# One mask for a pair of index tiles, and the buffers given up for a third pair

## The chip, the cores and the metric

The kernel runs on one core of a Trainium2 chip. The core has engines with queues of their own: TensorE (PE in the profile, its weight loads PEld), VectorE (DVE), ScalarE (ACT), GpSimd (POOL) and SyncE (SP), whose queue issues every DMA of this kernel. Each engine runs its instructions in the order in which they were written; they wait for each other through semaphores. The metric is the device time of one execution, in microseconds.

## The reference

32 audio clips of 313 frames go through one layer. A tokenizer (a DCT of each frame of 512 samples), an attention layer with eight heads, and a feed-forward layer of another kind than usual: each of 256 hidden units has its own wavelength and phase for each of the 512 features, and its output is a weighted sum over the features of sines and cosines from a table with 4096 entries.

```python
def lookup_sin_cos(theta):
    idx = jnp.mod(jnp.round(theta * (4096 / TWO_PI)), 4096).astype(jnp.int32)
    return sin_t[idx], cos_t[idx]

def ffn(x, W, B_param, attn_cos, attn_sin, proj_cos_w, proj_sin_w):
    theta = x[..., None, :] / (1.0 + jnp.abs(W)) + B_param     # (clip, frame, 256, 512)
    sin_theta, cos_theta = lookup_sin_cos(theta)
    cos_sum = jnp.sum(cos_theta * attn_cos, axis=-1)
    sin_sum = jnp.sum(sin_theta * attn_sin, axis=-1)
    return silu(einsum('bsn,dn->bsd', cos_sum, proj_cos_w)
                + einsum('bsn,dn->bsd', sin_sum, proj_sin_w))

h = dct(frames(x))
h = h + attention(layernorm(h))        # rotated Q and K, softmax times a decay matrix, V,
                                       # a norm per head, a SiLU gate, an output matrix
h = h + ffn(layernorm(h))
```

With 32 x 313 x 256 x 512 angles, and a sine and a cosine of each, the feed-forward layer is most of the work.

## The kernel before, in words

**Sines.** Features lie on the 128 partitions, in four groups of 128 (`NC4`). For one hidden unit and one group, VectorE turns the layernormed features of several clips into int16 table indices with one multiply-add (L610); unit and feature set two scalars of each partition. A tile of indices holds 16 blocks (`SLOT`) of one clip's 313 frames: with 8 clips at hand, two (unit, group) parts; with 4 clips four parts, with 2 clips eight, and with 6 clips two parts, which is 12 blocks. Three more VectorE instructions follow over the whole tile: `mask` (L622) wraps the index into the table and flips its top bit, `quarter` (L630) adds a quarter of the table into a second tile, and `wrap` (L636) wraps that. ScalarE takes the sine of each tile (L643) into a float32 tile `trig`; the second of the two sines is the cosine. TensorE multiplies each block by a 128 x 32 matrix that is zero outside one unit's column of weights (`hot`, loaded at L592), and so sums over features in PSUM banks `pa` (L664). One tile of indices and its partner is called a step below: 2144 of them.

**Rounds.** A ring holds the features of up to four pairs of clips. A round takes 32 units (`UNITS`) for all that are in it; a pair of clips stays for eight rounds. The ring fills slowly: one pair for four rounds, two for six, three for four, four from round 14 on, and it empties in the last six rounds. At a round's end the sums leave through `part` (L681) to device memory (L692), and when a pair of clips has all its sums, `output` projects them and adds the residual.

**Attention.** The attention of each clip (a sequence) is woven into the rounds as features are needed. Two sequences, A and B, run before the first round, with ScalarE taking the copies; so do those that fall in rounds with one pair in the ring. The others use VectorE for them. A sequence does: DCT by `rows` (L273: 12 products, one load of the ring of weights per three), layernorm, transposes (L260), V by `rows`, then twice four heads: Q and K and their swapped copies by `columns` (L288), the rotation (L341, L345, L346), scores (L355), maximum (L363), difference (L372), exponentials (L379, L384), sums (L397), and for each head transposes (L412), product with the decay table (L424) and with V (L430); then gate, norm per head, output matrix, residual (L502) and the second layernorm. GpSimd runs three Newton steps of four instructions for each inverse root (L224 to L227) between a seed on VectorE (L218) and the normalising instruction (L248, L484).

**Order.** The order of every engine's instructions is worked out before the build by the class `Plan`. Each piece of work is added with a key, an engine, an estimated duration, and what it reads and writes. `emit` runs through time on those estimates: on the engine that is free first it issues the ready piece with the lowest key. A DMA's data is taken to arrive 3500 ns after its issue (`LAND`). Keys come from the rounds' progress, and attention's keys are spread so that it is done when its clips enter the ring. The estimates set only the order; on the chip the waits decide the times.

**Buffers.** `ix` 4 index tiles, `trig` 3, `hot` 2 (two units, four groups each), a ring of 3 weight tiles, 2 decay tables, `h` for rows and values, `xn` for layernormed rows, `prob` for four heads, `probT`.

Of the kernel before, what the change touches and what calls it, by code (L numbers as in the profile page):

```python
# [21 lines left out]
P = 128  # L22
# [104 lines left out]
def tile_audio_tower(ctx: ExitStack, tc: tile.TileContext, t: dict, out: bass.AP):  # L127
# [7 lines left out]
    N_RING = 3  # L135
    N_IX, N_TRIG, N_HOT, N_PA = 4, 3, 2, 4
# [15 lines left out]
    class Buffers:  # L152


        def __init__(self, name, pool, psum):
            self.name = name
            self.n_ring = 0

# [4 lines left out]
            self.dec = [sb(f"dec{i}", STEP * (NT - 1) + S) for i in range(2)]  # L163

            self.u = sb("u", NC4, S)
            self.qk = [self.u[:, 2 * i : 2 * i + 2, :] for i in range(2)]
            self.h = sb("h", NT, HOP)
            self.v = self.h
            self.xn = sb("xn", NT, HOP)
            self.xnT = sb("xnT", NC4, S)  # L170
            self.prob = sb("prob", NB, NT, S)
            self.probT = sb("probT", NT, S)
            self.raw = self.probT[:, 0:2, :]
            wide = self.prob.rearrange("p a b s -> p (a b s)")
            self.sq = wide[:, : NT * HOP].rearrange("p (i d) -> p i d", d=HOP)
# [36 lines left out]
    def rsqrt(plan, key, val, r, u, kv, kr, ku):  # L212
# [17 lines left out]
        plan.add(key, "POOL", 3500, newton, (kv,), (kr, ku))  # L230

    def layernorm(plan, key, x):

        for i in range(NT):
            def stats(i=i):
                nc.vector.bn_stats(x.st[:N, i, :], x.h[:N, i, :])  # L236
                nc.vector.bn_aggr(x.mv[:N, i, :], x.st[:N, i, :])
            plan.add(key, "DVE", 850, stats, (x.k("h"),), (x.k("mv", i),))
# [6 lines left out]
        for i in range(NT):  # L245
# [3 lines left out]
                    x.xn[:N, i, :], x.h[:N, i, :], x.mv[:N, i, 0:1], x.lr[:N, i : i + 1],  # L249
                    ALU.subtract, ALU.mult,  # L250
                ),
                (x.k("h"), x.k("mv", i), x.k("lr")), (x.k("xn", i),),
            )

    def transposed(plan, key, x):

        for c in range(NC4):
            def go(c=c):
                for i in range(NT):
                    nc.tensor.transpose(  # L260
                        x.W[:, c, ROW0[i] : ROW0[i] + N], x.xn[:N, i, c * P : (c + 1) * P],
                        ident[:N, :N],
                    )
            plan.add(key, "PE", 800, go, x.every("xn", NT), x.banks(c))
# [28 lines left out]
    def attention(plan, keys, sq, x, eng):  # L293
# [9 lines left out]
        def residual(key, load):  # L303
            for i in range(NT):
                f0 = 1 if i and not load else 0
                d, s = h_d[sq, ROW0[i] + f0 : ROW0[i] + N, :], x.h[f0:N, i, :]
                kd, ks = ("h_d", sq), x.k("h")
                if load:
                    plan.add(key, "SP", DMA_NS, lambda d=d, s=s: nc.sync.dma_start(s, d), (kd,), (ks,))
                else:  # L310
                    plan.add(key, "SP", DMA_NS, lambda d=d, s=s: nc.sync.dma_start(d, s), (ks,), (kd,))

        xns, probs, us = x.every("xn", NT), x.every("prob", NB), x.every("u", 2)
# [3 lines left out]
        copy(plan, step(), eng, NT * HOP, x.h[:N], W3, x.banks(0, 1, 2), (x.k("h"),))  # L317
# [8 lines left out]
        copy(plan, step(), eng, NT * HOP, x.v[:N], W3, x.banks(0, 1, 2), (x.k("h"),))  # L326
        plan.add(step(0), "POOL", 500, lambda: nc.gpsimd.memset(x.v[0:1, : NT - 1, :], 0.0), (),
                 (x.k("h"),))

        for hb in range(H // NB):  # L330
            for g in range(hb * NB // 2, (hb + 1) * NB // 2):
# [8 lines left out]
                plan.add(key, "DVE", 810,  # L340
                         lambda qk=qk: nc.vector.tensor_tensor(qk, x.W[:, 0:2, :S], cos_qk, ALU.mult),  # L341
                         x.banks(0, 1), (kq,))

                def turned(qk=qk):
                    nc.vector.tensor_tensor(x.raw, x.W[:, 2:4, :S], sin_qk, ALU.mult)  # L345
                    nc.vector.tensor_tensor(qk, qk, x.raw, ALU.add)  # L346
                plan.add(key, "DVE", 1640, turned, x.banks(2, 3), (x.k("probT"), kq))
            for hd in range(hb * NB, (hb + 1) * NB):
# [16 lines left out]
                if a == NB - 1:  # L365
# [9 lines left out]
                         (x.k("mx", hd % 2), *x.banks(0, 1, 2)), (x.k("prob", a),))  # L375

            def exps(hb=hb, m=m):
                if eng == "DVE":
                    nc.scalar.activation(x.prob[:N, : NB - 1], x.prob[:N, : NB - 1], AF.Exp)  # L379
                for a in range(NB):  # L380
                    for i in range(NT):
                        last = a == NB - 1
                        if last or eng == "ACT":
                            nc.scalar.activation(  # L384
                                x.prob[:N, a, i, :],
                                x.W[:N, i, :S] if last else x.prob[:N, a, i, :], AF.Exp,
# [567 lines left out]
```

## Time and profile before

| | |
|---|---|
| time, median of 3 runs | 18,893.47 us (18,890.79 to 18,904.49) |
| the profiled execution | 18,894.1 us |
| its span, first to last instruction | 18,892.3 us |
| granted TensorE clock, mean | 0.926 |
| ACT busy | 18,090.3 us (96%), of it sines (L643) 17,547.6 |
| DVE busy | 17,770.2 us (94%), of it index work (L610, L622, L630, L636) 15,729.2 |
| PE busy | 14,803.3 us (78%) |
| POOL busy | 656.5 us (3%) |
| DMA | 783.69 MB, 41 GB/s |

A line of a group gives the kernel line, engine, operation, the tile written and those read with their sizes, how often, then busy time and mean ns of one, then the idle time of that engine just before and what ended it. A line of a wait gives engine, tile and line that waited, what it waited for, total us, times, and the longest. A line of the timeline gives start, duration and the work, and in brackets how long the engine stood before it. Matmuls in float32 appear as two records each.

### The profile page before, as it was taken

How to read it: one execution, taken by the hardware profiler on the slowest of the kernel's cores; microseconds unless marked ns; L12 is line 12 of the kernel's file. 1: busy time of each engine (PE TensorE's matmuls, PEld its weight loads, DVE VectorE, ACT ScalarE, POOL GpSimd, SP SyncE). 2: the span in 40 equal slices, each digit the busy share in tenths (PEclk: the TensorE clock that was granted, in tenths of full speed). 3: DMA queues.
4: the chain of work that ended last, by engine and by line, in shares of the span. 5: the costliest groups of instructions: out<-in, count | busy, mean ns of one | idle time of the engine just before them, and what ended most of it. 6: DMA issues, size and time to landing. Idle time of an engine off the chain costs nothing.

```text
span 18892.3 us, 332980 instructions
## 1 busy us (share of the span) xinstructions
PE 14803.3 (78%) x148864; PEld 6590.0 (35%) x148864; DVE 17770.2 (94%) x15244; ACT 18090.3 (96%) x5026; POOL 656.5 (3%) x1222
## 2 busy tenths in 40 slices
PE   8888888887888887888788888887888788766566
PEld 4433333333333333333333333333333333222222
DVE  5999999999999999999999999999999999889998
ACT  3899999999999999999999999999999999999998
POOL 0000000000000000000000000000000000000000
PEclk8999999999999999999999999999999999889998
DMA  3211111111111111111111111111111111000011
GB/s 96 66 52 48 50 57 47 46 51 47 31 35 37 46 42 41 32 40 46 38 45 39 32 44 41 45 40 36 39 38 46 39 45 35 24 10 25 12 30 46
DMA packets 447834, 783.69 MB, mean 41 GB/s; under 512 B 61601, under 2 KB 116129, under 8 KB 446401
## 3 DMA queue, kind: packets, MB, share of 16 engines
q1 hardware_dynamic: 446400, 762.39, 13.3%
q8 instruction: 1167, 19.12, 0.4%
q14 instruction: 267, 2.18, 0.0%
HBM read 657.51 MB, written 104.66 MB: 40 GB/s over the span
## 4 chain that ended last, share of the span: by engine, by line
DVE 55%; ACT 18%; PE 15%; issue 8%; POOL 3%; DMA 1%; DVEq 0%; SPq 0%; ACTq 0%; POOLq 0%
DVE ix L610 20%; ACT trig L643 18%; DVE ix L630 9%; DVE ix L622 9%; PE pa L664 8%; DVE ix L636 8%; PE a_W L288 3%; PE a_W L273 2%; DVE a_mx L363 1%; DVE a_prob L372 1%; DVE a_sm L397 1%; DVE a_probT L424 1%; DVE a_st L236 1%; PE a_W L355 1%; POOL a_lu L224 1%
## 5 line engine op out<-in xcount | busy, mean ns | idle before, releaser
L643 ACT ACTIVATE trig<-ix 128x5008 f32<-128x5008 int16 (+1 forms) x4288 | 17547.6, 4178 | 442.0 <-PE pa L664 185.5
L664 PE MATMUL pa<-trig,hot 128*32 128x313 f32 x131072 | 10373.1, 462 | 3021.0 <-ACT trig L643 3003.0
L664 PEld LDWEIGHTS pa<-trig,hot 128*32 128x32 f32 x131072 | 4058.5, 116 | 8907.0 <-ACT trig L643 4513.9
L610 DVE TENSOR_SCALAR ix<-xT,f 128x2504 int16<-128x2504 f32 (+3 forms) x5888 | 6673.8, 1184 | 211.9 <-ACT trig L643 205.8
L630 DVE TENSOR_SCALAR ix<-ix 128x5008 int16<-128x5008 int16 (+1 forms) x2144 | 3014.4, 1406 | 201.2 <-DVE ix L622 5.0
L622 DVE TENSOR_SCALAR ix<-ix 128x5008 int16<-128x5008 int16 (+1 forms) x2144 | 3023.7, 1410 | 69.2
L636 DVE TENSOR_SCALAR ix<-ix 128x5008 int16<-128x5008 int16 (+1 forms) x2144 | 3017.3, 1407 | 67.2
L288 PE MATMUL a_W<-a_xnT,a_ring 128*128 128x313 f32 x4960 | 1539.2, 446 | 220.1 <-DVE a_u L341 125.1
L273 PE MATMUL a_W<-a_ring,a_u 128*105 128x512 f32 x2256 | 1101.5, 623 | 120.8 <-DVE a_u L499 53.7
L288 PEld LDWEIGHTS a_W<-a_xnT,a_ring 128*128 128x128 f32 x4960 | 882.9, 191 | 868.2 <-issue 284.7
L430 PE MATMUL a_W<-a_h,a_probT 105*105 105x64 f32 x4464 | 540.6, 270 | 118.0 <-DVE a_probT L424 117.7
L273 PEld LDWEIGHTS a_W<-a_ring,a_u 128*105 128x105 f32 x2256 | 360.2, 174 | 722.8 <-issue 579.0
L430 PEld LDWEIGHTS a_W<-a_h,a_probT 105*105 105x105 f32 x4464 | 476.3, 181 | 386.4 <-issue 194.7
L355 PE MATMUL a_W<-a_u 64*105 64x313 f32 x1488 | 502.8, 466 | 112.0 <-DVE a_prob L372 100.6
L412 PE MATMUL a_W<-ident,a_prob 105*105 105x105 f32 x2232 | 325.9, 284 | 186.7 <-ACT a_prob L384 150.9
L273 PE MATMUL a_W<-a_ring,a_xnT 128*105 128x512 f32 x744 | 380.0, 631 | 50.9 <-DVE a_xnT L210 49.3
L224 POOL TENSOR_TENSOR a_gu<-a_gr 105x24 f32<-105x24 f32 x93 | 69.5, 747 | 10066.3 <-DVE a_gr L218 10061.4
L412 PEld LDWEIGHTS a_W<-ident,a_prob 105*105 105x105 f32 x2232 | 259.4, 185 | 344.9 <-ACT a_prob L384 193.2
L260 PE MATMUL a_W<-ident,a_xn 105*128 105x105 f32 x1116 | 190.2, 298 | 234.8 <-DVE a_xn L248 108.2
L355 PEld LDWEIGHTS a_W<-a_u 64*105 64x105 f32 x1488 | 239.3, 178 | 386.0 <-DVE a_prob L372 152.6
L363 DVE TENSOR_REDUCE a_mx<-a_W 105x3 f32<-105x939 f32 x248 | 280.2, 1130 | 17.7 <-PE a_W L355 17.1
L424 DVE TENSOR_TENSOR a_probT<-a_W,a_dec 105x939 f32<-105x939 f32 x248 | 279.9, 1129 | 13.0 <-PE a_W L412 13.0
(136 smaller groups left out, 3461.9 us busy)
## 6 DMA issues: line engine op xcount, KB each, us to landing
hot<-in_hot SPq DMA_DIRECT2D x672, 256.0 KB
a_dec<-in_decay SPq DMA_DIRECT2D x248, 260.5 KB
a_ring<-in_proj SPq DMA_DIRECT2D x128, 256.0 KB
a_ring<-in_dct SPq DMA_DIRECT2D x124, 256.0 KB
a_ring<-wv_d SPq DMA_DIRECT2D x124, 256.0 KB
a_ring<-in_wq SPq DMA_DIRECT2D x124, 256.0 KB
a_ring<-in_wk SPq DMA_DIRECT2D x124, 256.0 KB
a_ring<-in_wq_s SPq DMA_DIRECT2D x124, 256.0 KB
```

The costliest lines, as they stand in the source:

```text
L273: lambda c=c, i=i, k=k, to=to: nc.tensor.matmul(x.W[:N, to, :], lhsT[:, c, ROW0[i] : ROW0[i] + N], x.ring[k], start=(c == 0), stop=(c == N ...
L288: lambda c=c: nc.tensor.matmul(x.W[:, bank, :S], w[:, c, :], x.xnT[:, c, :], start=(c == 0), stop=(c == NC4 - 1)),
L355: lambda i=i, qk=qk, r0=r0: nc.tensor.matmul(x.W[:N, i, :S], qk[r0 : r0 + DH, 0, ROW0[i] : ROW0[i] + N], qk[r0 : r0 + DH, 1, :], start=Tru ...
L363: lambda m=m: nc.vector.tensor_reduce(m[:N], x.W[:N, :NT, :S], AX.X, ALU.max),
L412: nc.tensor.transpose(x.W[:N, jj, ROW0[i] : ROW0[i] + N], x.prob[:N, a, i, ROW0[j] : ROW0[j] + N], ident[:N, :N],)
L430: nc.tensor.matmul(x.y[:N, i, (hd % 2) * DH : (hd % 2 + 1) * DH], x.probT[:N, jj, ROW0[i] : ROW0[i] + N], x.v[:N, jj, hd * DH : (hd + 1) * ...
L610: nc.vector.tensor_scalar(now["ix", x][:, d0 : d0 + 2 * m * S], now["xT", c][:, 2 * at * S : 2 * (at + m) * S], f[:, 0, c, n + u : n + u + ...
L622: nc.vector.tensor_scalar(tl, tl, LUT - 1, LUT // 2, ALU.bitwise_and, ALU.bitwise_xor)
L630: nc.vector.tensor_scalar(tl[:, :E], now["ix", xs][:, :E], float(LUT // 4), None, ALU.add)
L636: nc.vector.tensor_scalar(tl, tl, LUT - 1, None, ALU.bitwise_and)
L643: nc.scalar.activation(tl[:, :E], now["ix", x][:, :E], AF.Sin, bias=-PI32, scale=ANG)
L664: nc.tensor.matmul(now["pa", p][g * 32 : g * 32 + 32, :S], now["hot", z][:, u, c, k, :], now["trig", w][:, s0 : s0 + S], start=(n == 0 and ...
```

## The change

The three instructions over index tiles become two. `quarter` writes its sum to the second half of a double tile from the unmasked first half, and one `mask` then wraps and flips both halves. The tiles are made once, three double ones in place of four single ones. Room comes from elsewhere: layernorm normalises rows in place, so `xn` is gone, and one buffer `h` holds rows, values and each head's result, tracked in four column groups; `prob` keeps three heads and the fourth's exponentials go to `probT`, so heads are taken in the order 3, 2, 0, 1; one decay table in place of two, two ring tiles in place of three, one `f` table in place of two. `hot` is split into halves of two groups, three of them. The rotation is one product of four column blocks with a joint table `turn_qk`, and one sum. The residual is loaded back after the transposes of the normed result, not before the gate. The planner's estimate for the Newton steps is 6000 ns in place of 3500.

```diff
-    N_RING = 3
-    N_IX, N_TRIG, N_HOT, N_PA = 4, 3, 2, 4
+    N_RING = 2
+    N_IX, N_TRIG, N_HOT, N_PA = 3, 3, 3, 4
...
-            self.dec = [sb(f"dec{i}", STEP * (NT - 1) + S) for i in range(2)]
+            self.dec = sb("dec", STEP * (NT - 1) + S)
...
-            self.xn = sb("xn", NT, HOP)
...
-            self.prob = sb("prob", NB, NT, S)
+            self.prob = sb("prob", NB - 1, NT, S)
...
+            self.exp = [*(self.prob[:, a] for a in range(NB - 1)), self.probT]
+            self.turn = wide[:, NT * S : NT * S + 4 * S].rearrange("p (i s) -> p i s", s=S)
...
-        plan.add(key, "POOL", 3500, newton, (kv,), (kr, ku))
+        plan.add(key, "POOL", 6000, newton, (kv,), (kr, ku))
...
-                    x.xn[:N, i, :], x.h[:N, i, :], x.mv[:N, i, 0:1], x.lr[:N, i : i + 1],
+                    x.h[:N, i, :], x.h[:N, i, :], x.mv[:N, i, 0:1], x.lr[:N, i : i + 1],
...
-                plan.add(key, "DVE", 810,
-                         lambda qk=qk: nc.vector.tensor_tensor(qk, x.W[:, 0:2, :S], cos_qk, ALU.mult),
-                         x.banks(0, 1), (kq,))
...
-                    nc.vector.tensor_tensor(x.raw, x.W[:, 2:4, :S], sin_qk, ALU.mult)
-                    nc.vector.tensor_tensor(qk, qk, x.raw, ALU.add)
+                         lambda: nc.vector.tensor_tensor(
+                             x.turn, x.W[:, :, :S], turn_qk, ALU.mult),
+                         x.banks(0, 1, 2, 3), probs[1:])
+                plan.add(key, "DVE", 870,
+                         lambda qk=qk: nc.vector.tensor_tensor(
+                             qk, x.turn[:, 0:2], x.turn[:, 2:4], ALU.add),
+                         probs[1:], (kq,))
...
-            for hd in range(hb * NB, (hb + 1) * NB):
+            for hd in (hb * NB + a for a in (3, 2, 0, 1)):
...
-                         lambda hd=hd, d=d: nc.sync.dma_start(x.dec[d], t["decay"][hd]),
-                         (), (x.k("dec", d),))
+                         lambda hd=hd: nc.sync.dma_start(x.dec, t["decay"][hd]),
+                         (), (x.k("dec"),))
...
-        residual(step(0), True)
...
         transposed(plan, step(4), x)
+        residual(step(0), True)
...
+            for n, c in dict.fromkeys((n // 2 * 2, c // 2 * 2) for n, c in parts):
+                if (n, c) in hot:
+                    continue
+                z = hot[n, c] = place("hot", N_HOT)
...
+                             new("hot", z, [P, 2, 2, 2, 32], bufs=N_HOT),
+                             t["hot"][:, blk * UNITS + n : blk * UNITS + n + 2, c : c + 2]),
...
-                            nc.vector.tensor_scalar(
-                                tl, tl, LUT - 1, LUT // 2, ALU.bitwise_and, ALU.bitwise_xor)
-                        plan.add(key, "DVE", 130 + 0.26 * E, mask, (), (("ix", x),))
...
-                            tl = now["ix", x][:, :E]
-                            nc.vector.tensor_scalar(tl, tl, LUT - 1, None, ALU.bitwise_and)
-                        plan.add(key, "DVE", 130 + 0.26 * E, wrap, (), (("ix", x),))
...
+            def quarter(x=x, E=E):
+                tl = now["ix", x]
+                nc.vector.tensor_scalar(tl[:, 1, :E], tl[:, 0, :E], float(LUT // 4), None, ALU.add)
+            plan.add(key, "DVE", 220 + 0.26 * E, quarter, (("ix", x, 0),), (("ix", x, 1),))
+
+            def mask(x=x, E=E):
+                tl = now["ix", x][:, :, :E]
+                nc.vector.tensor_scalar(
+                    tl, tl, LUT - 1, LUT // 2, ALU.bitwise_and, ALU.bitwise_xor)
+            plan.add(key, "DVE", 220 + 0.26 * 2 * E, mask, (), [("ix", x, i) for i in range(2)])
...
+        for x in range(N_IX):
+            new("ix", x, [P, 2, SLOT * S], I16, bufs=N_IX)
```

## The prediction

> **What bounds the kernel now.** The busy shares come first: ScalarE (ACT) 96%, VectorE (DVE) 94%, TensorE 78%. Two engines so close cannot be told apart by an average, so I cut the span into stretches by the number of clips in the ring. Columns after the stretch: its length, then busy time and instructions of PE, PEld, DVE, ACT, POOL; then clock and DMA.
>
> ```profile
> 350.00:1000.00 650.00, 532.27 (x4820) 270.78 (x4812) 609.38 (x801) 557.56 (x238) 36.15 (x75) 0.90 0.22 64
> 1000.00:5000.00 4000.00, 3247.32 (x31636) 1487.81 (x31640) 3827.03 (x3595) 3756.20 (x1147) 168.30 (x317) 0.94 0.16 48
> 5000.00:16300.00 11300.00, 9096.99 (x92176) 4026.20 (x92164) 10788.86 (x8155) 11173.17 (x2857) 432.80 (x747) 0.93 0.13 40
> 16300.00:18000.00 1700.00, 1049.71 (x12688) 395.09 (x12688) 1558.52 (x1420) 1693.62 (x462) 0.00 (x0) 0.92 0.05 15
> 18000.00:18800.00 800.00, 530.67 (x5928) 203.21 (x5920) 783.48 (x1011) 787.13 (x187) 0.00 (x0) 0.90 0.12 37
> ```
>
> ACT idles 92 us in the first stretch, 244 in the second, 127 in the third, 6 in the fourth, 13 in the fifth. The change takes no sine away (ACT's 18,090 us stay), so these 482 us and some 320 before and after them are all that could be won. Who withholds them is in the waits, here of ACT in the second stretch (first three lines), ACT in the third (next three), and DVE over the whole run.
>
> ```profile
> ACT trig L643 <- DVE ix L622: 100.9, 71, 4.1
> ACT trig L643 <- PE pa L664: 69.6, 36, 5.2
> ACT trig L643 <- DVE ix L636: 41.3, 22, 2.8
> ...
> ACT trig L643 <- PE pa L664: 54.0, 27, 3.8
> ACT trig L643 <- DVE ix L636: 27.5, 27, 2.5
> ACT a_xn L531 <- PE a_W L273: 25.9, 11, 3.9
> ...
> DVE ix L610 <- ACT trig L643: 205.8, 264, 2.7
> DVE a_xn L248 <- POOL a_lr L227: 150.4, 62, 3.3
> DVE a_xn L484 <- POOL a_gr L481: 72.0, 30, 2.9
> ```
>
> In the second stretch DVE is busy 95.7% and waits for ACT only 5.9 us in all: DVE binds. A second saved on it there is a second off the end, up to ACT's 244 us. The first stretch is alike (DVE 93.8%). In the third ACT binds, at 98.9%.
>
> **The joint mask.** Call a step one tile of indices, 16 x 313 values, with two sines (4.27 us apart, so 8.53 us of ACT). On DVE it has one to eight index instructions, then three over the tile:
>
> ```profile
> L630 DVE TENSOR_SCALAR ix<-ix 128x5008 int16<-128x5008 int16 x1760 | 2576.0, 1464 | 163.7 <-DVE ix L622 4.6 <-ACT trig L643 3.7
> L630 DVE TENSOR_SCALAR ix<-ix 128x3756 int16<-128x3756 int16 x384 | 438.4, 1142 | 37.5 <-DVE ix L622 0.5 <-ACT trig L643 0.3
> ```
>
> The slope is 322/1252 = 0.257 ns per value, the fixed part 1464 - 5008 x 0.257 = 176 ns; L622 gives 149. The change runs one instruction over 10,016 values in place of two over 5008, so it saves one fixed part: 0.16 us of 7.5 to 8.7 us of DVE per step. [...]
>
> L630 counts the steps. First stretch 59: 9 us. Second 485: 78. Third: nothing of itself, for ACT binds. Fourth: nothing. Last rounds, with eight short index instructions a step:
>
> ```profile
> 18209.86 4.21 DVE L610 TENSOR_SCALAR ix<-xT,f 128x626 int16<-128x626 f32 x8
> ...
> 18218.56 4.22 DVE L610 TENSOR_SCALAR ix<-xT,f 128x626 int16<-128x626 f32 x8
> ```
>
> From start to start 8.70 us against ACT's 8.53: DVE binds, and 96 such steps (64 with two clip pairs apart in the ring, 32 with one) give 96 x 0.16 = 15 us.
>
> **Rotation and sums in attention.** Three instructions (L341, L345, L346: 804 + 806 + 812 ns) become one of 1252 columns from PSUM (the copy of that shape, L210, takes 1455) and one of 812: 0.155 us less, four times a sequence. The sums are 2 x 2102 before, 1130 + (1130 + 2 x 972) = 4204 after: nothing. With 2 sequences in the first stretch and 8.5 in the second: 1 and 5 us.
>
> **POOL's longer estimate.** Each normalising step waits about 2.4 us for GpSimd's Newton chain, and the planner is now told 6000 ns, not 3500. The trace shows what that buys:
>
> ```profile
> 7484.79 1.39 POOL L224 TENSOR_TENSOR a_lu<-a_lr 105x3 f32<-105x3 f32 x1 [77.72 <-DVE a_lr L218]
> 7486.26 1.42 POOL L225 TENSOR_TENSOR a_lu<-a_lu,a_lv 105x3 f32<-105x3 f32 x1
> 7487.76 1.41 POOL L226 TENSOR_SCALAR a_lu<-a_lu 105x3 f32<-105x3 f32 x1
> 7489.26 0.19 POOL L227 TENSOR_TENSOR a_lr<-a_lr,a_lu 105x3 f32<-105x3 f32 x1
> ...
> 7491.69 1.46 DVE L248 TENSOR_SCALAR a_xn<-a_h,a_mv,a_lr 105x512 f32<-105x512 f32 x3 [2.57 <-POOL a_lr L227]
> ```
>
> While DVE runs its index work, one GpSimd instruction passes per DVE instruction, at 1.4 us; once DVE stands waiting, the rest take 0.19, one each 0.275 us. In the instruction order of before three DVE instructions lie between seed and normalising, so nine remain: 9 x 0.275 = 2.5, as measured. In that of the changed kernel mostly four lie there (two index, quarter, joint mask): eight remain, 2.2 us. So 0.3 us each, not 2.5: 26 of them in the second stretch give 8 us, the 6 of the first 2. [...]Were nothing let through until DVE stops, the wait would be the prologue's 3.4 us whatever lies between, and the 10 us would be nil. The row shows one instruction slipping in per DVE instruction; I keep 10.
>
> **Third tile of pairs.** Lookahead grows from two steps to three. Where DVE binds, it is never ahead, and depth gives nothing. In the third stretch it bridges attention's bursts on DVE: I take all 30 us that ACT waits there for L636 and L622.
>
> **Two ring buffers.** In the order of before TensorE runs up to 12 row products (L273; a chain piece of 24 records takes 10.48 us, two records each) between two sines' products. In that of the changed kernel never more than 6, since the third load waits for a buffer: 5.2 us. ACT has three trig tiles: after a sine ends, its products (2.31 us) may be 2 x 4.27 - 2.31 = 6.2 us late before ACT stands. 10.5 overshoots by 4.3, 5.2 by nothing. Of the 54 us in the third stretch I take 40 (bounds 0 and 54); the row products before L531 stay.
>
> **What it costs.** In place, normalising must wait until the raw rows are stored. In steady work some 12 us lie between (statistics 2.5, seed 0.5, four DVE instructions 7.4, the POOL wait), against 1.3 of issue and a landing of 2 to 4 (sums land 2.05 us after their issue ends; SP waits at most 4.3 for a 626 KB store). In the prologue the third store is issued at 36.61 us, behind ring loads on SP, and the normalising of 35.0 waits: +4. Ring reloads and the single decay table add some 6 there: +10 (0 to 30). At the end the last two row products wait up to 1.2 us per load: +3. The single decay table elsewhere: its reload starts when the head before is done, and index instructions worth 12 us or more lie between two heads in the new order: nothing. The residual's reload, moved behind the last transposes, precedes L502 by two steps of attention: nothing. Hot pieces double to 1344 issues of 0.33 us on a queue that mostly waits. Attention starts each sequence within two steps of where it did. For SP being late now and then on DVE's new waits I add 11 (0 to 60).
>
> **Sum.** First stretch 9 + 1 + 2 = 12, second 78 + 5 + 8 = 91, third 30 + 40 = 70, last 15: 188. Less 10 + 3 + 11: 164. The profiled execution took 18,894.1 us (span 18,892.3 and 1.8 around it), 0.6 above the median of 18,893.5. So 18,730.
>
> **Rivals.** (1) More: with shorter bursts DVE's real waits in the first two stretches (27 and 89 us, its idle time less the 2.1% that it has between records in the fifth stretch) and all 127 of the third vanish: (10 + 27) + (83 + 89) + 127 + 15 - 24 = 327, 18,567. For it: attention's chain loses long blocks on TensorE. Against: 60 of those 89 are DVE's waits for POOL, and they stay. (2) The change doesn't do what it says: the long mask costs two short ones, and bursts on TensorE are made up elsewhere. Left are 16 + 30, less 24: 18,872. For it: only two shapes fix the fixed part. (3) Slower, by one mechanism: the hot tile while one pair of clips is in the ring. A step then needs two half tiles of three, so one is reloaded between the first half of one sine's products and the second half of the next, 4.3 us. A loop of reload plus 2.3 us of products beats 8.53 once issue to landing exceeds 6.2 us; each microsecond more costs 96 us over the 96 steps. It outweighs 164 from 7.9 us on; at 9 it ends at +105: 19,000. Against: landings above are 2 to 4 us. For it: SP is one queue, and in the first stretch it stands 138 us at decay loads and 156 at ring loads.
>
> **Numbers.** Chances: forecast 0.64 (own range 18,660 to 18,800), rival 1 0.17, rival 2 0.09, rival 3 0.10. A difference under 0.2%, 38 us, cannot be told from none with this kernel. Faster 0.84 (forecast, rival 1, a third of rival 2), same 0.07 (the rest of it, a little of rival 3), slower 0.09. The range of 18,600 to 18,880 leaves out rival 3 and half of rival 1.
>
> **What would show it.** The joint mask at 2.75 to 2.8 us, one per step; DVE busy down by some 350 us with ACT's 18,090 unchanged; 1000 to 5000 us holding some 12 steps more; DVE still waiting about 2.2 us for POOL at each normalising; ACT's waits for L664 in the third stretch down to some 15 us; no DMA among DVE's long waits. It is wrong if the mask takes 5 us, if normalising or the decay product waits for a DMA, or if ACT idles in the second stretch for TensorE instead of DVE.

## The result, and the profile after

The changed kernel takes 18,693.05 us (median of 4 runs, 18,689.40 to 18,696.15), the kernel before 18,895.19 us beside it. The ratio is 0.9892, 95% interval 0.9878 to 0.9906: 202 us faster. The forecast was 18,730 us, a gain of 164 us.

The busy times by stretch, in the columns of the table of before (the fourth and fifth stretch start earlier, since the work is further on):

```profile
350.00:1000.00 650.00, 517.25 (x4586) 265.49 (x4586) 590.13 (x725) 538.81 (x233) 42.58 (x64) 0.89 0.20 59
1000.00:5000.00 4000.00, 3270.68 (x32531) 1526.19 (x32531) 3852.88 (x3152) 3856.22 (x1177) 279.28 (x329) 0.94 0.17 49
5000.00:16300.00 11300.00, 9089.69 (x93124) 4017.19 (x93124) 10696.08 (x6860) 11292.37 (x2883) 602.01 (x747) 0.94 0.13 40
16300.00:17800.00 1500.00, 905.79 (x11224) 343.89 (x11224) 1347.26 (x1108) 1498.78 (x416) 0.00 (x0) 0.95 0.05 16
17800.00:18600.00 800.00, 540.89 (x5920) 205.90 (x5924) 777.95 (x932) 784.80 (x188) 0.00 (x0) 0.87 0.13 37
```

In the third stretch ScalarE (fourth pair of numbers) is now busy 11,292 of 11,300 us: nothing is left there. In the second it is busy 3856 us instead of 3756, in the first 539 instead of 558.

The waits that answer to those of before: ScalarE's in the second stretch (two lines), in the third (two lines), and VectorE's over the whole run (four lines).

```profile
ACT trig L644 <- PE pa L666: 62.0, 40, 6.3
ACT trig L644 <- DVE ix L636: 55.4, 41, 3.7
...
ACT trig L644 <- PE pa L666: 2.5, 3, 0.9
ACT a_h L543 <- PE a_W L277: 1.5, 1, 1.5
...
DVE ix L631 <- ACT trig L644: 485.3, 583, 5.9
DVE a_h L252 <- POOL a_lr L231: 108.2, 58, 2.3
DVE a_h L495 <- POOL a_gr L492: 50.4, 30, 2.3
DVE ix L619 <- DMA xT<-xT_d: 31.3, 11, 13.2
```

In the third stretch ScalarE's waits for TensorE fell from 54.0 to 2.5 us, and the 25.9 us at the output's activation (L531, now L543), which the forecast let stand, to 1.5. VectorE stands 485 us for ScalarE at the quarter (L631), 405 of them in the stretch with four clip pairs; before, it stood 206 us at the index (L610). So it has more often become the engine that is ahead, and it now waits at another instruction of the step. The experiments below turn on that.

The joint mask in its two shapes:

```profile
L636 DVE TENSOR_SCALAR ix<-ix 128x10016 int16<-128x10016 int16 x1760 | 4872.9, 2769 | 55.5
L636 DVE TENSOR_SCALAR ix<-ix 128x7512 int16<-128x7512 int16 x384 | 814.1, 2120 | 12.0
```

**Where the 202 us came from.** A cut at fixed times mixes different work, so from here on stretches are cut at the starts of the same sines (number 1, 128, 512, 1024, 3840, 4096, 4288), in each kernel's profiled execution. The first three stretches (64, 192 and 256 steps, one to three clip pairs in the ring) stand as one, since attention is shifted between them.

| stretch | before | after | gain | forecast |
|---|---|---|---|---|
| up to the first sine | 331.2 | 353.9 | -22.7 | -10 |
| first 512 steps | 4360.3 | 4268.0 | 92.3 | 12 + 91 |
| 1408 steps with four pairs | 12,475.3 | 12,345.4 | 129.9 | 70 |
| last 224 steps | 1677.5 | 1670.7 | 6.8 | 15 |
| after the last sine's start | 48.0 | 49.6 | -1.6 | -3 |

### The profile page after: what moved, and what is told of

Its sections match the earlier page's. It is cut to its first block, busy times and chain, and to the rows that moved or that the text cites. A ratio compares the mean times of both kernels' runs of the same rounds, so it can differ in the third digit from the quotient of the medians.

```text
span 18687.6 us, 332496 instructions
## 1 busy us (share of the span) xinstructions
PE 14667.1 (78%) x148864; PEld 6569.4 (35%) x148864; DVE 17425.4 (93%) x12972; ACT 18069.0 (97%) x5026; POOL 944.3 (5%) x1222
## 5 line engine op out<-in xcount | busy, mean ns | idle before, releaser
L666 PE MATMUL pa<-trig,hot 128*32 128x313 f32 x131072 | 10264.9, 458 | 3322.3 <-ACT trig L644 3268.9
L636 DVE TENSOR_SCALAR ix<-ix 128x10016 int16<-128x10016 int16 (+1 forms) x2144 | 5687.0, 2653 | 67.5
L631 DVE TENSOR_SCALAR ix<-ix 128x5008 int16<-128x5008 int16 (+1 forms) x2144 | 3029.4, 1413 | 622.0 <-ACT trig L644 485.3
L228 POOL TENSOR_TENSOR a_lu<-a_lr 105x3 f32<-105x3 f32 x186 | 145.4, 782 | 3833.3 <-DVE a_lr L222 3823.5
L264 PE MATMUL a_W<-ident,a_h 105*128 105x105 f32 x1116 | 182.8, 293 | 158.0 <-DVE a_h L252 77.1
L424 PE MATMUL a_W<-ident,a_prob 105*105 105x105 f32 x1674 | 243.2, 276 | 15.8 <-DVE a_h L456 15.8
L345 DVE TENSOR_TENSOR a_prob<-a_W,turn_qk 128x1252 f32<-128x1252 f32 x124 | 180.4, 1455 | 73.5 <-PE a_W L292 37.3
```

The lines of the kernel that those rows point to most:

```text
L424: nc.tensor.transpose(x.W[:N, jj, ROW0[i] : ROW0[i] + N], x.exp[a][:N, i, ROW0[j] : ROW0[j] + N], ident[:N, :N],)
L631: nc.vector.tensor_scalar(tl[:, 1, :E], tl[:, 0, :E], float(LUT // 4), None, ALU.add)
L636: nc.vector.tensor_scalar(tl, tl, LUT - 1, LUT // 2, ALU.bitwise_and, ALU.bitwise_xor)
L666: nc.tensor.matmul(now["pa", p][g * 32 : g * 32 + 32, :S], now["hot", hot[n - u, c // 2 * 2]][:, u, c % 2, k, :], now["trig", w][:, s0 : s ...
```

## The experiments

All starts of sines below are from one profiled execution of each kernel; times and ratios are medians of the runs against the kernel before on the same chip. Where the profiled execution is far from the median, the stretches do not add to the difference of the medians. In the names of the runs, "pairs" are double index tiles (two halves each) and "rings" the weight tiles of attention's products; "the four-pair stretch" is the one with four pairs of clips, 1408 steps. The stretches first, for all (us):

| kernel | to the first sine | 512 steps | 1408 steps | last 224 | end | ratio to before, interval |
|---|---|---|---|---|---|---|
| before | 331.2 | 4360.3 | 12,475.3 | 1677.5 | 48.0 | |
| changed | 353.9 | 4268.0 | 12,345.4 | 1670.7 | 49.6 | 0.9892 (0.9878 to 0.9906) |
| e1: two pairs | 345.0 | 4297.5 | 12,453.8 | 1662.7 | 52.7 | 0.9953 (0.9941 to 0.9966) |
| e2: two masks | 352.7 | 4303.7 | 12,378.8 | 1675.3 | 54.2 | 0.9922 (0.9909 to 0.9936) |
| e3: three rings | 350.1 | 4273.7 | 12,366.8 | 1679.6 | 47.7 | 0.9906 (0.9892 to 0.9919) |
| e4: four half tiles | 353.1 | 4258.3 | 12,351.7 | 1660.2 | 55.3 | 0.9877 (0.9862 to 0.9892) |
| e5: two pairs, three rings | 340.8 | 4313.9 | 12,486.9 | 1674.9 | 48.4 | 0.9989 (0.9982 to 0.9995) |
| e6: before, two rings | 333.3 | 4355.0 | 12,453.0 | 1669.6 | 54.3 | 0.9979 (0.9971 to 0.9986) |
| e7: estimate 3500 | 347.0 | 4280.6 | 12,348.5 | 1672.5 | 53.4 | 0.9898 (0.9884 to 0.9911) |
| e8: e5 with two masks | 339.4 | 4329.2 | 12,474.0 | 1679.6 | 46.7 | 0.9986 (0.9980 to 0.9993) |
| e10: e5, mask first | 349.6 | 4351.2 | 12,438.4 | 1683.9 | 47.2 | 0.9979 (0.9971 to 0.9988) |
| e11: e4 with two f | 346.5 | 4253.0 | 12,349.0 | 1660.2 | 52.0 | 0.9873 (0.9858 to 0.9888) |
| e12: changed again | 356.1 | 4269.5 | 12,349.2 | 1672.4 | 53.1 | 0.9890 (0.9876 to 0.9903) |

The changed kernel profiled twice agrees within 4 us in every stretch. No run leaves out any of the computation.

**e1, two tiles of pairs**

```diff
-    N_IX, N_TRIG, N_HOT, N_PA = 3, 3, 3, 4
+    N_IX, N_TRIG, N_HOT, N_PA = 2, 3, 3, 4
```

> The changed kernel with two tiles of index pairs instead of three. In the changed kernel the stretch with four clip pairs (1408 steps) is 130 us shorter than before, against 70 forecast, and ScalarE idles 8 us in it. Forecast's theory: the third pair removed about 30 us of waits for VectorE there; with two pairs these come back, so +30 us (18,723), all in that stretch, and the stretches with two and three pairs stay (VectorE binds, depth gives nothing there). Rival theory: the third pair, not the shorter row bursts, bridges nearly all of attention's work on VectorE; then +100 us or more (18,790 or above), with ScalarE waiting for the mask or the index instructions for 80 us or more in that stretch and for longer in the two before it.

Measured: 18,813.47 us. It lies 88 below before instead of 202, so 114 us of the gain are gone. The four-pair stretch alone is 108 longer, and the first 512 steps are 30 longer, where the forecast's theory expected no loss. ScalarE's waits in the four-pair stretch:

```profile
ACT trig L644 <- DVE ix L636: 98.9, 70, 4.2
ACT trig L644 <- PE pa L666: 10.0, 15, 1.2
```

The rival holds: the third pair is the largest part of the gain. But 99 us of waits for VectorE are far more than the 37 us (L636, L622 and L610) that the kernel before had there, which also had room for two steps. Something in the change took lead away.

**e2, the mask as two instructions**

```diff
-            def mask(x=x, E=E):
-                tl = now["ix", x][:, :, :E]
+            for i in range(2):
+                def mask(x=x, E=E, i=i):
+                    tl = now["ix", x][:, i, :E]
...
-            plan.add(key, "DVE", 220 + 0.26 * 2 * E, mask, (), [("ix", x, i) for i in range(2)])
+                plan.add(key, "DVE", 220 + 0.26 * E, mask, (), [("ix", x, i)])
```

> The changed kernel with the joint mask taken apart into two instructions over one half each (three pairs, short rings and all else as changed). Forecast's theory: a mask of half length takes 1464 ns, two cost 0.16 us a step more than the 2769 ns of the joint one; the stretches in which VectorE binds give that back: with two and three pairs of clips 448 steps x 0.16 = 72 us, one-pair stretch and last rounds up to 24 more, the four-pair stretch nothing: +72 to +96 us (18,765 to 18,789). Rival: ScalarE is the bound nearly everywhere once three pairs are there, and the mask saved nothing: within 20 us of the changed kernel (18,713 or below).

Measured: 18,755.69 us, so 56 us of the gain are gone. The profiled execution, at 18,766.51 the slowest of the four, is 36 longer in the first 512 steps, 33 in the four-pair stretch and 5 in the last 224 steps. Neither theory expected this. But this edit undoes less than both took for granted, as VectorE's timeline shows (two records of L637 in one line):

```profile
12008.30 1.47 DVE L631 TENSOR_SCALAR ix<-ix 128x5008 int16<-128x5008 int16 x1
12009.80 2.84 DVE L637 TENSOR_SCALAR ix<-ix 128x5008 int16<-128x5008 int16 x2
12012.55 3.07 DVE L619 TENSOR_SCALAR ix<-xT,f 128x2504 int16<-128x2504 f32 x2
```

Each half takes 1463 ns, yet both together take 2.84 us, not 2.93: they do not depend on each other, and the second begins before the first has ended. From start to start, as medians over 6000 to 16,000 us, a step of the four-pair stretch is on VectorE

| | index (2) | then, each to the next start | sum |
|---|---|---|---|
| before, mask 1.57, quarter 1.50, wrap 1.38 | 3.11 | 4.45 | 7.56 |
| e2, quarter 1.50, two masks 2.75 | 3.18 | 4.25 | 7.43 |
| changed, quarter 1.50, joint mask 2.68 | 3.18 | 4.18 | 7.36 |

So the change saves 0.20 us a step, 0.13 by the new order and 0.07 by the joint instruction, and e2 takes back 0.07. 512 x 0.07 = 36: in the first 512 steps its full price, as the forecast's theory has it. In the four-pair stretch a third of 1408 x 0.07 = 99 shows, where it expected nothing.

**e3, three ring tiles**

```diff
-    N_RING = 2
+    N_RING = 3
```

> The changed kernel with three ring tiles instead of two. Forecast's theory: TensorE's blocks of row products grow again to as many as twelve between two sines' products; the 40 us of ScalarE's waits for TensorE come back in the four-pair stretch, and the prologue, where TensorE waited 16 us at ring loads, gets 6 to 16 us shorter: +24 to +34 us (18,717 to 18,727). Rival: the third pair of index tiles (VectorE ahead of ScalarE) gave the whole four-pair gain and the bursts didn't matter: nothing in that stretch, the prologue 6 to 16 us shorter, so 18,677 to 18,687.

Measured: 18,726.84 us, so 27 us of the gain are gone. By the profiled executions the four-pair stretch is 21 longer and the last 224 steps, where `output` has its row products, 9; the prologue is 4 shorter, where 6 to 16 were expected. In the four-pair stretch ScalarE's waits for the sines' products are 15.5 us instead of 2.5, and those at the output's activation (L543) 7.5 instead of 1.7. The forecast's mechanism is there, at 13 us of waits against its 40.

**e4, four half tiles of the hot matrix**

```diff
-    N_IX, N_TRIG, N_HOT, N_PA = 3, 3, 3, 4
+    N_IX, N_TRIG, N_HOT, N_PA = 3, 3, 4, 4
```

> The changed kernel with four half tiles of the hot matrix in place of three. The one-pair stretch at the start became 23 us longer where 12 shorter was forecast, and the last 96 steps gave 1 us where 15 was forecast. Theory of the hot reload (the slower rival in part): TensorE stands for the half tile, ScalarE's waits for TensorE at the start (78 us) and TensorE's 20.6 us of waits in the last rounds go, so the start gains 20 to 35 us and the last rounds 10 to 15: 18,643 to 18,663. Rival: the start is longer because attention's chain now has more ends that wait (two ring tiles, layernorm in place behind stores), and the last rounds because VectorE is at ScalarE's pace anyway: within 8 us of the changed kernel, 18,685 or above.

Measured: 18,673.67 us, between the two expectations and 26 us less than the changed kernel by the differences to before; the intervals overlap. The last rounds in the changed kernel, from the timeline around the end of a round (SPq is SyncE's queue):

```profile
18512.16 1.18 SPq L695 DMA_DIRECT2D sums_d<-part  x2
18513.44 1.04 SPq L609 DMA_DIRECT2D hot<-in_hot  x2
18514.53 2.39 SPq L695 DMA_DIRECT2D sums_d<-part  x4
...
18515.88 5.71 PE L666 MATMUL pa<-trig,hot 128*32 128x313 f32 x64 [11.86 <-DMA hot<-in_hot]
...
18518.32 8.65 ACT L644 ACTIVATE trig<-ix 128x5008 f32<-128x5008 int16 x2 [7.09 <-PE pa L666]
```

The half tile itself lands 2.4 us after its issue begins (13.44 to 15.88). It is late because its issue stands on SyncE's queue behind the stores of the round's sums, which wait for VectorE's copies. TensorE stood 11.9 us, and through it ScalarE 7.1. Over the last 96 steps TensorE's waits for half tiles were 20.6 us in the changed kernel; with four half tiles there is none, and those 96 steps take 829.1 us instead of 839.8 (before 841.2). So the 15 us forecast for the mask there are 12 once the reload is out of the way.

At the start the theory holds only in a small part. The one-pair stretch became 51 us shorter, but the next one 41 longer: with a fourth tile the planner puts less of attention ahead of the sines (268 records of row products by the 128th sine, against 295). Moved work looks like a gain until the next stretch is read too; the two together gained 11.

**e5, both depths undone**

```diff
-    N_RING = 2
-    N_IX, N_TRIG, N_HOT, N_PA = 3, 3, 3, 4
+    N_RING = 3
+    N_IX, N_TRIG, N_HOT, N_PA = 2, 3, 3, 4
```

> The changed kernel with both depths undone: two tiles of index pairs and three ring tiles. Alone, two pairs cost 108 us in the four-pair stretch and three ring tiles 21. Theory that the two causes are separate (each fills its own waits, VectorE's and TensorE's): they add, the four-pair stretch is 130 us longer than in the changed kernel, 12,475, as before. Forecast's sizes: 30 + 40, 12,415. Rival (one covers for the other): with two pairs ScalarE stands for VectorE wherever it would stand for TensorE too, so long row bursts cost little more once two pairs are there: 12,454 to 12,465; or, the other way round, without the third pair's lead every long burst is felt: above 12,500.

Measured: 18,877.81 us, a mere 21 below before (0.9982 to 0.9995), although the joint mask and the new rotation are in it. The four-pair stretch is at 12,487, 12 above before. The costs of the two depths nearly add here: 108 (e1) and 21 (e3), against 141 together. ScalarE's waits there, and VectorE's over the whole run:

```profile
ACT trig L644 <- DVE ix L636: 105.1, 65, 3.9
ACT trig L644 <- PE pa L666: 28.5, 21, 2.4
...
DVE ix L631 <- ACT trig L644: 638.6, 790, 8.8
```

Both wait for each other: VectorE 639 us at the quarter, and ScalarE behind it for the mask.

**e6, the kernel before with two ring tiles**

```diff
-    N_RING = 3
+    N_RING = 2
```

> The kernel before with two ring tiles instead of three and nothing else. Forecast's theory: row bursts of at most six products take 40 of the 54 us of ScalarE's waits for TensorE out of the four-pair stretch, at 6 us more in the prologue: 18,860 on the first run's scale, that stretch 12,435. Rival: ScalarE stands for TensorE because VectorE hands attention's tiles on late there, and burst length is not the cause: the stretch stays within 10 us of 12,475 and the time within 15 of before or above it, since row products now wait for their loads too.

Measured: 18,855.07 us, 44 below before (0.9971 to 0.9986). In the profiled execution, the slowest of the 15 at 18,866.97, the four-pair stretch is 22 shorter, the last 224 steps are 8 shorter and the prologue is 2 longer. ScalarE's waits for the sines' products in the four-pair stretch went from 54.0 to 41.9 us, those at L531 from 25.9 to 2.8. So two ring tiles gain by themselves, in the stretch as much as in e3 (21), which is half of the 40 forecast. By the waits most of it comes from the output's row products (23 us), which the forecast had let stand, and 12 from the sines' products, on which it counted.

**e7, the planner's old estimate for GpSimd**

```diff
-        plan.add(key, "POOL", 6000, newton, (kv,), (kr, ku))
+        plan.add(key, "POOL", 3500, newton, (kv,), (kr, ku))
```

> The changed kernel with the planner's old estimate of 3500 ns for the GpSimd chain in place of 6000. Forecast's theory: one VectorE instruction fewer lies between seed and normalising, each wait of VectorE for GpSimd (1.7 to 1.9 us now) is 0.3 us longer, 26 of them in the stretches with two and three pairs and few elsewhere: +10 us, not to be told from the changed kernel by its time, but by its waits. [...]Rival: the estimate moves enough of attention to put instructions elsewhere, more than 20 us either way.

Measured: 18,706.49 us, 10 to 17 above the changed kernel by the differences to before (192 against 202 and 209), which the intervals can't tell from nothing; the first 512 steps are 11 to 13 longer. VectorE's waits for GpSimd in the four-pair stretch, changed kernel first, then with 3500:

```profile
DVE a_h L252 <- POOL a_lr L231: 85.6, 40, 2.3
...
DVE a_h L495 <- POOL a_gr L492: 29.5, 20, 2.0
```

```profile
DVE a_h L252 <- POOL a_lr L231: 90.8, 40, 2.6
...
DVE a_h L495 <- POOL a_gr L492: 60.5, 20, 3.5
```

The norm per head waits 3.0 us instead of 1.5, the layernorms 2.27 instead of 2.14. So the waits do depend on what lies between. Had GpSimd been let through only once VectorE stands, the case that the prediction weighed, they would have been equal.

**e8, old depths and two masks**

The edits of e2 and e5 together.

> Two index pairs, three ring tiles and the mask as two half instructions: of the change there remain the joint rotation, layernorm in place, half tiles of the hot matrix, three kept heads and single buffers. Forecast's theory: rotation and GpSimd chain give 16, prologue and end cost 13: 18,890 on the first run's scale, and the mask is worth 102 us against the run with the same depths and the joint mask, none of it in the four-pair stretch. Rival: the mask is worth as much in the four-pair stretch as elsewhere, since with two pairs VectorE's lead there is short and 0.16 us a step shortens its waits: 30 us or more there.

Measured: 18,873.46 us, 4 us below e5, which is neither theory. With the old depths joining two neighbouring masks is worth nothing in the time: by the profiled executions it gains 15 us, of a price of 36, in the first 512 steps, and loses 13 in the four-pair stretch. The whole step from three instructions to two is not undone here either, since the two masks stay side by side behind the quarter; e10 undoes it.

**The lost lead.** The traces of e1, e5 and e8 suggested a reason, which e10 tests. Call lead the time that attention may hold VectorE before ScalarE has to wait. The sizes that follow are estimates, worked out from the durations of the rows. Before, a step ran index, mask, quarter, wrap. The index waits for the sine that frees its tile; from then on ScalarE has three more sines, 12.8 us, and its next half is ready after index and mask, 3.07 + 1.47 = 4.5 us. Attention may thus hold VectorE for 8.3 us. In the changed order the first sine waits for quarter and joint mask, 1.47 + 2.77 = 4.2 us, and the quarter waits for the *second* half's sine, after which ScalarE has only two sines, 8.5 us: 4.3 us are left with two pairs, 4.3 + 8.5 = 12.8 with three. The sizes are rough: in e8 the first sine waits for only one of the two masks, which leaves 8.5 - 1.47 - 1.46 = 5.6 us, yet its waits for the masks in the four-pair stretch are 114.4 us, no less than the 105.1 of e5.

**e9, e5 once more**, as an anchor (the label's words do not describe it: its edit is that of e5).

> A second look at the run with two pairs and three ring tiles, as an anchor for the next: both theories expect the four-pair stretch at 12,487 within 15 us and ScalarE's waits for the joint mask there at some 105 us.

Measured: 18,875.27 us in a single execution, beside 18,907.96 for the kernel before. The four-pair stretch is at 12,485.0 and ScalarE's waits for the joint mask there at 106.9, both as expected. The other stretches are within 4 us of e5, except the prologue: 351.9 against 340.8 us, for the same program.

**e10, two pairs with the mask first**

e5 with the steps in the order of before, in halves of the joint tile. The planner's estimates of the three instructions go back too (160 instead of 220 in the quarter's), so the place of attention's work in the order may move with them:

```diff
+            def mask(x=x, E=E):
+                tl = now["ix", x][:, 0, :E]
...
+            plan.add(key, "DVE", 130 + 0.26 * E, mask, (), [("ix", x, 0)])
             def quarter(x=x, E=E):
...
-            def mask(x=x, E=E):
-                tl = now["ix", x][:, :, :E]
...
+            def wrap(x=x, E=E):
+                tl = now["ix", x][:, 1, :E]
+                nc.vector.tensor_scalar(tl, tl, LUT - 1, None, ALU.bitwise_and)
+            plan.add(key, "DVE", 130 + 0.26 * E, wrap, (), [("ix", x, 1)])
```

> Two index pairs and three ring tiles as in the two runs with the old depths, but per step index, mask of the first half, quarter, wrap of the second, as before the change: the first sine's half is ready one instruction after the index. Theory of the lost lead (formed after the runs so far): from the end of the sine that frees a half, ScalarE has three sines, 12.8 us; index and mask take 4.5, which leaves 8.3 us for attention on VectorE. With the joint mask the first sine waits for quarter and joint mask behind the second half's release: 8.5 less 4.2, 4.3 us. That is why ScalarE's waits for VectorE in the four-pair stretch rose from 37 us before to 105 with two pairs and the joint mask. It expects the waits for VectorE back at 35 to 50 us and the stretch 40 to 70 us below the 12,487 with the joint mask. Rival (the tiles are freed two by two, or half tiles of the hot matrix and layernorm in place make VectorE's bursts longer): waits stay near 110 us and the stretch within 15 us of 12,474.

Measured: 18,866.52 us, 41 below before, against 21 for e5 in its comparison and 33 for e9's single execution: undoing the step from three instructions to two costs nothing at these depths, and may gain 9 to 20 us, which the intervals do not separate. ScalarE's waits in the four-pair stretch (L631 is now the mask of the first half, L642 the wrap, and VectorE waits at the index again):

```profile
ACT trig L649 <- PE pa L671: 51.7, 25, 4.8
ACT trig L649 <- DVE ix L631: 25.1, 24, 2.4
ACT a_h L543 <- issue: 15.3, 7, 4.6
...
ACT trig L649 <- DVE ix L642: 1.5, 2, 0.8
...
DVE ix L619 <- ACT trig L649: 180.8, 227, 3.4
```

Waits for VectorE fell from 105 to 27 us, below the 35 to 50 expected, and the stretch by 48 us, inside the 40 to 70 expected, with half tiles, in-place layernorm and tiles in pairs unchanged. Waits for TensorE's sums rose by 23 and those at the output's activation (L543) by 11, which is why the 78 are not all won. So it is the order of the step, with the quarter ahead of the mask of the first half, that costs the four-pair stretch its time at these depths. The first 512 steps became 37 us longer than in e5, and the last 224 by 9. There a step costs VectorE 7.56 us again (medians of its timeline: 3.11, 1.57, 1.50, 1.38), 0.20 more than in e5, and that counts, though not at its full 102 in the 512 steps. The order with the mask first was not tried with three pairs.

**e11, four half tiles and two tiles of frequencies**

e4, and

```diff
-        fz = place("f", 1)
+        fz = place("f", 2)
```

with `bufs=2` at its tile.

> The changed kernel with four half tiles of the hot matrix and two tiles of frequencies. Theory of the reloads at round boundaries: the first index instruction of a round no longer waits for the load of the frequencies (2 to 3 us in the last rounds, nothing that shows elsewhere), so 2 to 6 us below the run with four half tiles alone, 18,668 to 18,672 on the first run's scale, 25 to 35 below the changed kernel in the same call. Rival: those waits lie beside ScalarE's work; within 3 us of the run with four half tiles alone.

Measured: 18,665.54 us (18,657.17 to 18,671.73), and beside it the changed kernel 18,698.65 (18,686.11 to 18,707.87): 33 us less, with ranges that do not touch. This version beats both kernels. How much of it the second `f` tile gives is not settled. The last 96 steps take 829.1 us in both e4 and e11, so VectorE's wait for `f` there (2.5 us in e4) lay beside ScalarE's work. What remains is 5 us in the first 512 steps and 7 us in the prologue, where two executions of one program differ by 11 (e5 and e9).

**e12, the changed kernel again**

> The changed kernel once more, beside the run with four half tiles and two tiles of frequencies, so that the two stand on the same chip: both theories expect 18,690 to 18,705.

Measured: 18,698.65 us, ratio 0.9890: as in the result, and the anchor of e11.

## Why the prediction was right, and where it was not

The time came out 37 us below the forecast, inside its own range, and most of its signs are there: the mask at 2.77 us; VectorE's busy time 345 us lower (17,770.2 to 17,425.4) and ScalarE's at 18,069; 497 steps in 1000 to 5000 us, 12 more than 485; waits for TensorE in the third stretch down to 2.5. One sign of being wrong half came: in the second stretch ScalarE now waits longer for TensorE (62.0 us) than for the mask (55.4), though less for both than before (69.6 for TensorE and 142.2 for VectorE's two masks). Rival 1 was right of the third stretch, where 119 of ScalarE's 127 idle us went, and wrong of the second, where 144 of 244 stayed.

The sum hides parts that were wrong. From before to after one part at a time, by the table of stretches:

| part | first 512 steps | 1408 steps | last 224 |
|---|---|---|---|
| before to e10: rotation, GpSimd's estimate, in place, half tiles, order | -9 | -37 | +6 |
| e10 to e5: three index instructions to two | -37 | +48 | -9 |
| e5 to e1: two ring tiles | -16 | -33 | -12 |
| e1 to changed: third pair | -30 | -108 | +8 |
| sum | -92 | -130 | -7 |
| forecast, in the same order | -16, -87, 0, 0 | 0, 0, -40, -30 | 0, -15, 0, 0 |

In another order the parts differ: what one edit is worth depends on those already in. By this path the joint mask gives next to nothing where 102 us were forecast, and the third pair 130 where 30 were. That these two errors cancel is luck, and so is most of the nearness of the total. Of the first row, only GpSimd's estimate was tried alone (e7); where its 37 us in the four-pair stretch come from stays open.

**Joint mask, its price: near.** 2 x 1464 - 2769 = 159 ns by durations, against 160; from start to start the step is 0.20 shorter. The rows of the two shapes (L630 and L622 of before) gave it. The rotation's two instructions took 1455 + 811 ns, as forecast.

**Joint mask, its worth: wrong at the old depths.** The step that failed is "DVE binds. A second saved on it there is a second off the end", together with "Third: nothing of itself". Of 87 us forecast for the first two stretches it gives 37 (e10 to e5), and in the four-pair stretch it costs 48. Much of the time saved on VectorE became VectorE's wait. In the second stretch before, and in the same part of e5 (1056 to 4655 us), VectorE stands for ScalarE:

```profile
DVE ix L610 <- ACT trig L643: 5.9, 10, 1.3
```

```profile
DVE ix L631 <- ACT trig L644: 50.9, 77, 2.6
```

By the estimate from row durations, the new order took the first sine's lead from 8.3 to 4.3 us. With three pairs the forecast's step holds better: there the joining alone gives its full 36 in the first 512 steps (e2), and 33 in the four-pair stretch, where nothing was forecast.

**Third pair: wrong size and wrong place.** The forecast said "Where DVE binds, it is never ahead, and depth gives nothing", and for the third stretch "all 30 us that ACT waits there". The third pair gave 108 in the four-pair stretch with two rings and 120 with three (e5 to e3), and 30 in the first 512 steps. The 30 was read from the waits of the kernel before. With two pairs the new order waits more: the third pair had 105 us of ScalarE's waits to take away (e5), where the kernel before had 37.

**Two ring tiles: half the size, and in part another path.** They gave 21 to 33 us in the four-pair stretch (e3, e5 to e1, e6) where 40 were forecast. The waits for the sines' products, on which the 40 rested, fell by 12 (e6), 13 (e3) and 18 us (e5 to e1). The waits at L531, which were to "stay", fell too, from 25.9 to 2.8 in e6.

**GpSimd.** The waits fell from 2.4 to 1.9 (layernorm) and 1.7 us (norm per head); forecast 2.2. e7 agrees in sign and in size in the first 512 steps (11 to 13 for 10). The other case that the prediction weighed, in which nothing passes until VectorE stops, did not hold: with the old estimate the norm per head waits 3.0 us instead of 1.5 in the four-pair stretch (e7), and in the rows of the last section one GpSimd instruction passes per VectorE instruction.

**Costs.** The prologue cost 23 us where 10 were forecast, inside its bounds. The first row products of V begin at 50.8 us instead of 40.0: TensorE stood 6.4 us for the in-place normalising, whose third store is issued at 41.6 instead of 36.6 us (forecast 4), 1.2 more for the first load, and two ring loads at a time held the DCT's products. The other 12 lie after that: TensorE's 1028 records there take 263.8 us at a clock of 0.78, against 255.5 at 0.83, and e9 beside e5 shows the prologue of one program moving by 11 us with the clock (0.79 against 0.82). The sign "no DMA among DVE's long waits" failed once: 13.2 us for a clip's features (`xT`) as the second pair of clips enters.

**Last rounds: 1 us for 15, by a late half tile, as the third rival feared.** In the last 96 steps VectorE's step went from 8.70 to 8.50 us, below ScalarE's 8.53, as forecast. The late half tile took the gain, not as the loop of reload and products that the rival described (landing was 2.4 us, far from its 6.2), but as a queue: TensorE waited four times, the longest for an issue that stood behind stores. e4 and e11 gain 11 by removing it.

## What to carry to other kernels

Before an instruction over two buffers is joined, work out the lead of the producer: from the release it waits for to the first thing its consumer needs. A saving on the producer can be worth nothing if the consumer's first half now waits for a later release and more work (e10 to e5: 102 us forecast, none gained), until another buffer restores the lead (e1 to the changed kernel: 114 us). Waits in the profile of before price depth for the old order only, not for the order that the change makes.

Compare stretches cut at the same piece of work, and where other work may move across the cut, read the neighbours too (51 us gained and 41 given back in e4).

## What the runs showed of the hardware

In e2 and e8 the two masks of a step, on different halves of the tile, take 2.84 us together at 1.46 each: the second starts 1.38 us after the first, before that one ends. From quarter (1.47 us) to mask it is 1.50, so the mask starts behind the quarter's end. The quarter of the changed kernel shows both, 1.50 before the mask and 1.38 before another instruction (medians over 6000 to 16,000 us). Durations alone, with which the prediction worked, don't show these 0.12 us.

In the changed kernel a GpSimd instruction that begins beside VectorE's index work lasts until the VectorE instruction ends. At the layernorm of 12.0 ms (timeline, both engines):

```profile
12002.15 1.47 DVE L631 TENSOR_SCALAR ix<-ix 128x5008 int16<-128x5008 int16 x1
12002.18 1.49 POOL L230 TENSOR_SCALAR a_lu<-a_lu 105x3 f32<-105x3 f32 x1
12003.65 2.77 DVE L636 TENSOR_SCALAR ix<-ix 128x10016 int16<-128x10016 int16 x1
12003.75 2.72 POOL L231 TENSOR_TENSOR a_lr<-a_lr,a_lu 105x3 f32<-105x3 f32 x1
12006.55 0.19 POOL L228 TENSOR_TENSOR a_lu<-a_lr 105x3 f32<-105x3 f32 x1
```

Three instructions of one size take 1.49, 2.72 and, with VectorE standing, 0.19 us. Of the 480 GpSimd arithmetic instructions of that trace that begin beside an index, quarter or joint mask, 479 end 0.04 to 0.10 us after it, the median one 0.05. So one GpSimd instruction passes per VectorE instruction, and beside the joint mask that takes 2.7 us; GpSimd's busy time rose from 656 to 944 us with the same number of instructions.

The clock of TensorE in the prologue differs between executions of one program. In e5 its 1088 records took 282.7 us at a granted clock of 0.82, in e9 294.4 us at 0.79, and the first sine came 11.1 us later. A few us of difference in this prologue therefore say nothing about an edit.
